# A macaron network on one core: causal mask by VectorE, one product per scan tile, dt rows by group

## The chip, the cores and the metric

The kernel runs on one core of one Trainium2 chip. TensorE (PE in the profile) multiplies matrices, VectorE (DVE), ScalarE (ACT) and GpSimd (POOL) work elementwise, and nearly all transfers are issued from the queue of SyncE (SP). Each engine carries out its own instructions in the order in which they stand in its queue and waits at semaphores for the others. Time is the device time of one execution in microseconds (us); lower is better. Before the change the median of three runs was 1147.51 us.

## The reference

The input x has 4 batches of 512 tokens with 128 features. Six layers follow one another, each with a residual connection and a layer norm without weights in front:

```
x = x + 0.5 * tree_attention(layernorm(x))   # three 16-leaf tree MLPs give q, k, v; softmax attention
x = x + attention(layernorm(x))              # 16 heads of 8 features, RoPE, ALiBi, causal
x = x + 0.5 * tree_attention(layernorm(x))
x = x + 0.5 * experts(layernorm(x))          # 8 experts, top 2, and a shared one
x = x + mamba(layernorm(x))                  # selective scan, 256 channels, 16 states
x = x + 0.5 * experts(layernorm(x))
```

Two places matter here. In the causal attention the scores of keys after the query are replaced by a very negative number before the softmax:

```
scores = scores + slopes[:, None, None] * rel
scores = where(causal, -1e9, scores)
attn = softmax(scores)
```

In the scan each of 256 x 16 states obeys, along the 512 tokens,

```
dA = exp(dt[t] * A)
h  = dA * h + (dt[t] * x[t]) * B[t]
y  = sum over the 16 states of h * C[t]
```

## The kernel before, in words

One batch is four tiles of 128 tokens; most tiles are 128 partitions by 512 (`S`) fp32 elements. The work of each layer and batch is a Python generator that yields after each small step. `Job` objects give every step a due time from the table `TIMES` (`h0` to `h3` for the causal heads, `s0` to `s3` for the scan, `T`, `t`, `e`, `f` for trees and experts), and the steps are emitted in the order of those due times. So the heads of one batch are interleaved with trees and experts of others, and the scan of one batch with experts and trees of others. The framework that the kernel is written in then settles the order on each engine and inserts the semaphores. `work(role)` takes the next of `BUFS[role]` rotating SBUF buffers, `bank(role)` the next of `BANKS[role]` PSUM banks.

**Causal heads.** `head_consts` (L474) makes four stacks of queries (`qs`, role `q_bias`) and two of keys (`ks`, role `k_bias`), each filled with 1.0 by GpSimd (L480) and then given bias rows by DMA and ScalarE. `head_stack` (L526) moves the high and low parts of q and k into rows 24 to 119 of them, and `head_maxima` (L576) puts the negated row maxima into rows 120 to 127 of the query stacks, so that one matmul gives scores with ALiBi and with the maximum subtracted. `head_keys` (L536) makes, on GpSimd, four masked copies of the keys, one per head. `head_scores` (L546) runs a first round of score matmuls into the one bank of role `head_max` (L557) and lets VectorE take the masked row maximum (L565). `head_mix` (L590) runs the second round into two banks of role `head_sc` (L633), for four key tiles kt: queries before the key tile are left out, so that a view holds one head of 512 columns (kt=0), one of 384 (kt=1), two of 256 (kt=2) or four of 128 (kt=3), eleven views for each of 16 quarters (4 batches x 4), 176 views. In each view the first 128 columns of a head are the diagonal block. A matmul of an identity with a constant triangle in bf16, `future_t`, adds a large negative number to the masked part of all diagonal blocks of the view (L641), ScalarE takes the exponential into a `pt` tile (L649), and four steps later (`LAG_MIX`) matmuls with the values follow (L601).

**Selective scan.** `state_prep` (L830) computes dt, dt*x and B, C and writes the rows of dt and dt*x to DRAM (`state_rows`). `state_main` (L925) covers each batch with two chunks c of 128 channels. For a chunk, eight DMAs (`spread`, L923) bring for each of four groups g of 32 channels the rows of dt and of dt*x back, each row copied to four partitions (one per state), into `dts` and `dtxs` tiles of 4 x 512; there are two of each. Then for q = 0 to 3 (four states each) a matmul spreads B into a bank (L958), and for each g: ScalarE makes the decay (L970, two banks), VectorE multiplies dt*x by B (L971), VectorE scans (L972), GpSimd multiplies by C (L973). The scanned tiles are single 128 x 512 buffers of role `states`, eight of them. Five steps later (`LAG_STATE`) four matmuls add the states up (`sums`, L930, L934). In all there are 4 batches x 2 chunks x 4 q x 4 g = 128 such steps.

The constants for the mask come in one bf16 tile, `whole` (L200 to L203), with the leaf paths of the trees, the identity, `future_t` and `future`.

## Time and profile before

| what | value |
|---|---|
| median of three runs | 1147.51 us (1146.84 to 1148.99) |
| the profiled execution | 1150.85 us, span 1149.1 us |
| mean granted TensorE clock | 0.988 |
| PE busy | 1080.6 us (94%) |
| DVE busy | 909.7 us (79%) |
| ACT busy | 517.1 us (45%) |
| POOL busy | 411.6 us (36%) |
| DMA | 146.42 MB, mean 127 GB/s |

The time of an execution holds 1.75 us more than the span from the first to the last instruction. The profiled execution is 3.34 us above the median of the runs. PE rows give matmuls with modelled ends that overlap; PEld rows are weight loads beside them. A group's row in the profile has the instruction's line, engine, operation and tiles, its count, its busy time and mean duration, and then the idle time of the engine just before it and what ended most of it. In a window's row each engine has its busy time in that stretch and the number of instructions.

### The profile page before, as it was taken

What the parts mean: (1) busy time and instruction counts of PE and PEld (TensorE: products, weight loads), DVE (VectorE), ACT (ScalarE), POOL (GpSimd) and SP (SyncE); (2) the same over time, 40 slices, a digit from 0 to 9 for tenths busy, and PEclk for the clock granted to TensorE, in tenths of its full rate; (3) what the DMA queues carried; (4) which work ended last, traced back from release to release, by engine and by line L of the source; (5) the groups of instructions that cost most, each with busy time, mean ns of one, the idle gap of its engine ahead of it and who ended that gap; (6) DMA issues with size and microseconds to landing.
All of it is one profiled execution on the core that took longest, in us unless ns stands there. A gap on an engine that the chain in (4) does not pass through costs nothing.

```text
span 1149.1 us, 16519 instructions
## 1 busy us (share of the span) xinstructions
PE 1080.6 (94%) x5536; PEld 715.5 (62%) x5536; DVE 909.7 (79%) x2199; ACT 517.1 (45%) x1078; POOL 411.6 (36%) x396
## 2 busy tenths in 40 slices
PE   3999999999999999999999999998798989998998
PEld 2666566566665667765566676675276656655677
DVE  5566787577676677776789998799989999999864
ACT  2221423233332455544533643565476567454444
POOL 4115322002100141320314651266626656656623
PEclk9999999999999999999999999999899999999999
DMA  7787755231442122333752334662038323823310
GB/s 208 203 248 215 260 137 122 75 94 57 85 139 60 54 58 60 104 85 112 232 181 90 125 84 122 234 210 92 1 98 278 127 60 125 292 74 124 111 51 10
DMA packets 79653, 146.42 MB, mean 127 GB/s; under 512 B 7537, under 2 KB 39665, under 8 KB 79569
## 3 DMA queue, kind: packets, MB, share of 16 engines
q1 hardware_dynamic: 79280, 145.07, 42.1%
q8 instruction: 44, 0.72, 0.3%
q14 instruction: 41, 0.33, 0.1%
q10 hardware_dynamic: 288, 0.30, 0.1%
HBM read 125.35 MB, written 13.70 MB: 121 GB/s over the span
## 4 chain that ended last, share of the span: by engine, by line
PE 63%; DVE 20%; issue 6%; DMA 4%; POOL 3%; ACT 3%; SPq 1%; POOLq 0%; ACTq 0%; DVEq 0%
PE tree_acc L404 11%; PE moe_acc L773 7%; DVE states L972 6%; PE head_acc L601 5%; PE tree_mm L173 4%; PE head_max L557 4%; PE head_sc L633 3%; PE moe L173 3%; PE tree_mm L175 3%; PE tree_mm L174 3%; DVE states L971 3%; PE moe L174 3%; PE moe L175 3%; DVE u L759 2%; PE state_acc L934 2%
## 5 line engine op out<-in xcount | busy, mean ns | idle before, releaser
L973 POOL TENSOR_TENSOR states<-states,cs 128x512 f32<-128x512 f32 x128 | 163.4, 1282 | 161.9 <-DVE states L972 93.1
L404 PE MATMUL tree_acc<-full,ring 128*128 128x512 f32 x384 | 194.3, 598 | 5.2 <-DVE full L394 4.9
L565 DVE CUSTOM_DVE_ANT_0 head_max<-head_max,kept 128x128 f32<-128x128 f32 (+3 forms) x256 | 126.8, 496 | 64.1 <-PE head_max L557 61.9
L394 DVE SCALAR_TENSOR_TENSOR full<-tree_mm,kept,mask 128x512 f32<-128x512 f32 x188 | 138.5, 746 | 40.2 <-PE tree_mm L175 35.1
L649 ACT ACTIVATE pt<-head_sc 128x512 f32<-128x512 f32 (+1 forms) x176 | 95.0, 559 | 139.0 <-PE head_sc L641 138.3
L972 DVE TENSOR_TENSOR_SCAN states<-decay,states 128x512 f32<-128x512 f32 x128 | 154.6, 1216 | 0.5
L773 PEld LDWEIGHTS moe_acc<-ring,u 128*128 128x128 f32 x1152 | 141.4, 193 | 17.6 <-DVE u L765 3.0
L773 PE MATMUL moe_acc<-ring,u 128*128 128x128 f32 x1152 | 145.7, 278 | 1.0 <-DVE u L759 0.7
L173 PE MATMUL moe<-xl,ring 128*128 128x512 f32 x288 | 128.8, 448 | 8.9 <-DVE u L765 1.9
L784 POOL TENSOR_TENSOR kept<-kept,y 128x512 f32<-128x512 f32 x64 | 83.4, 1303 | 136.2 <-ACT y L783 118.8
L970 ACT ACTIVATE decay<-dts,kept 128x512 f32<-128x512 f32 x128 | 88.4, 693 | 88.1 <-DVE states L972 66.5
L758 ACT ACTIVATE u<-moe 128x512 f32<-128x512 f32 x144 | 86.3, 602 | 70.4 <-PE moe L175 66.5
L759 DVE SCALAR_TENSOR_TENSOR u<-u,moe 128x512 f32<-128x512 f32 x144 | 97.0, 677 | 23.4 <-ACT u L758 23.1
L174 PE MATMUL moe<-xh,ring 128*128 128x512 f32 x288 | 115.4, 401 | 0.0
L175 PE MATMUL moe<-xh,ring 128*128 128x512 f32 x288 | 115.0, 400 | 0.0
L541 POOL TENSOR_SCALAR km<-k_bias,kept 128x512 fp32r<-128x512 f32 x64 | 43.3, 697 | 171.3 <-PE head_sc L633 151.0
L783 ACT ACTIVATE y<-moe_acc,scratch 128x128 f32<-128x128 f32 x256 | 73.3, 370 | 65.6 <-PE moe_acc L773 64.8
L173 PE MATMUL tree_mm<-xl,ring 128*128 128x512 f32 x188 | 96.1, 514 | 0.4 <-DVE full L394 0.2
L404 PEld LDWEIGHTS tree_acc<-full,ring 128*128 128x128 f32 x384 | 71.0, 190 | 35.8 <-issue 17.3
L173 PEld LDWEIGHTS moe<-xl,ring 128*128 128x128 f32 x288 | 54.8, 190 | 60.4 <-DVE u L765 10.4
L557 PE MATMUL head_max<-km,q_bias 120*128 120x512 f32 (+2 forms) x192 | 91.7, 479 | 0.5 <-POOL km L541 0.4
L971 DVE TENSOR_TENSOR states<-state_b,dtxs 128x512 f32<-128x512 f32 x128 | 85.6, 682 | 5.5 <-PE state_acc L934 2.6
(242 smaller groups left out, 1982.3 us busy)
## 6 DMA issues: line engine op xcount, KB each, us to landing
ring<-moe_parts SPq DMA_DIRECT2D x72, 512.0 KB
ring<-tree_parts SPq DMA_DIRECT2D x42, 512.0 KB
ring<-in_fff_w SPq DMA_DIRECT2D x24, 512.0 KB
mask<-fff_taken SPq DMA_DIRECT2D x48, 256.0 KB
ring<-in_moe_w SPq DMA_DIRECT2D x16, 512.0 KB
dts<-state_rows SPq DMA_DIRECT2D x32, 256.0 KB
dtxs<-state_rows SPq DMA_DIRECT2D x32, 256.0 KB
moe_parts<-moe_w SPq DMA_DIRECT2D x9, 512.0 KB
```

The lines of the kernel that those rows point to most:

```text
L173: nc.tensor.matmul(ps, lhsT=lh, rhs=rl, start=start, stop=False)
L174: nc.tensor.matmul(ps, lhsT=ll, rhs=rh, start=False, stop=False)
L175: nc.tensor.matmul(ps, lhsT=lh, rhs=rh, start=False, stop=stop)
L394: nc.vector.scalar_tensor_tensor(full, ps, neg_b1[:, n : n + 1], st.masks[k][:, c, :], ALU.max, ALU.mult)
L404: nc.tensor.matmul(acc, lhsT=weights[k][1][:, c, :], rhs=h, start=(c == 0), stop=False)
L557: nc.tensor.matmul(view, lhsT=qs[:R_MAX, g, ts(i, P)], rhs=km[j0 // 2][:R_MAX, j0 % 2 : j0 % 2 + each, :kw], start=True, stop=True,)
L565: nc.vector.tensor_tensor_reduce(view[:, n, :], view[:, n, :], future[:, S - kw :], -1.0, float(np.finfo(np.float32).max), ALU.add, ALU.mi ...
L759: nc.vector.scalar_tensor_tensor(u, u, 1.0, ps1, ALU.add, ALU.mult)
L773: nc.tensor.matmul(acc[:, ts(i, P)], lhsT=h[c][:, ts(i, P)], rhs=w2[:, e % 4 * 2 + c, :], start=(c == 0), stop=(c == 1),)
L971: nc.vector.tensor_mul(h, bs, dtx[:, g, :])
L972: nc.vector.tensor_tensor_scan(h, dA, h, 0.0, ALU.mult, ALU.add)
L973: nc.gpsimd.tensor_mul(h, h, cs[:, q])
```

## The change: what it does

Four edits are made together.

- The mask. The identity matmul is gone. The score matmuls of a view are each a group of their own (start and stop), and VectorE replaces the diagonal blocks in PSUM by their minimum with a bf16 constant, `at_most`, which is a large negative number where the key comes after the query and 2^127 elsewhere. `whole` loses the identity.
- The product. For each q one VectorE instruction multiplies all four groups of `dtx` (128 x 4 x 512) by the bank with B, broadcast over the groups, into a `states` tile of 4 x 512. There are three such tiles. The scan, the product with C and the sums work on slices of it.
- The dt rows. `dts` is one 128 x 512 tile per group, six of them. `dtxs` stays two tiles of 4 x 512.
- The stacks. The four query stacks are not filled with 1.0 first; the two key stacks are.

```diff
-    ... dtx=2, pos=2, dts=2, dtxs=2, states=8),
+    ... dtx=2, pos=2, dts=6, dtxs=2, states=3),
...
-    whole = keep((3 * P + S) // 2).bitcast(BF16)
+    whole = keep((2 * P + S) // 2).bitcast(BF16)
...
-    leafpath, ident_h, future_t = (whole[:, ts(k, P)] for k in range(3))
-    future = whole[:, 3 * P :]
+    leafpath, at_most = (whole[:, ts(k, P)] for k in range(2))
+    future = whole[:, 2 * P :]
...
-                nc.gpsimd.memset(stack.bitcast(F32), 1.0)
+                if lst is ks:
+                    nc.gpsimd.memset(stack.bitcast(F32), 1.0)
...
                         rhs=qs[:, g, kt * P :],
-                        start=(j == 0),
-                        stop=False,
+                        start=True,
+                        stop=True,
                     )
-                nc.tensor.matmul(
+                nc.vector.tensor_tensor(
                     view[:, :, :P],
-                    lhsT=ident_h,
-                    rhs=future_t.unsqueeze(1).to_broadcast([P, each, P]),
-                    start=False,
-                    stop=True,
+                    view[:, :, :P],
+                    at_most.unsqueeze(1).to_broadcast([P, each, P]),
+                    ALU.min,
                 )
...
-                    rhs=hs[g],
+                    rhs=hs[:, g, :],
...
-            dt, dtx = work("dts", (4, S)), work("dtxs", (4, S))
+            dt, dtx = [], work("dtxs", (4, S))
...
             for g in range(4):
-                for m, to in enumerate((dt, dtx)):
-                    spread(to[:, g, :], rows[m, g])
+                dt.append(work("dts"))
+                for m, to in enumerate((dt[g], dtx[:, g, :])):
+                    spread(to, rows[m, g])
...
-                hs = []
+                hs = work("states", (4, S))
+                nc.vector.tensor_mul(hs, dtx, bs.unsqueeze(1).to_broadcast([P, 4, S]))
                 for g in range(4):
                     k = (4 * c + g) * GROUPS + q
-                    dA, h = bank("decay"), work("states")
-                    hs.append(h)
-                    nc.scalar.activation(dA, dt[:, g, :], AF.Exp, scale=A[:, k : k + 1])
-                    nc.vector.tensor_mul(h, bs, dtx[:, g, :])
+                    dA, h = bank("decay"), hs[:, g, :]
+                    nc.scalar.activation(dA, dt[g], AF.Exp, scale=A[:, k : k + 1])
                     nc.vector.tensor_tensor_scan(h, dA, h, 0.0, ALU.mult, ALU.add)
...
     k_after_q = np.triu(np.full((P, P), -FAR, f), 1)
+    at_most = np.where(k_after_q.T < 0, f(-FAR), f(2.0**127))
```

In the order of instructions on the engines the rest stays nearly where it was: apart from what is added and removed, most groups move by fewer than twenty places in queues of 1000 to 4000. The largest move is that of the transposes of one tree preparation, which stand some 260 PE instructions later, still ahead of the matmuls that use them. On SP the eight row loads of a chunk stand as two of dt, four of dt*x, two of dt, and in second chunks the last two of dt stand behind five to eight further loads, mostly of expert weights.

More of the change, by code (lines that the diff above doesn't have):

```diff
@@ L102 @@
     **dict(moe_w=1, lgT=1, u0=4, u1=3, y=2, v3=3),
-    **dict(hid=1, xs=3, sz=2, conv=1, xd=1, xb=2, cs=1, dt=3, dtx=2, pos=2, dts=2, dtxs=2, states=8),
+    **dict(hid=1, xs=3, sz=2, conv=1, xd=1, xb=2, cs=1, dt=3, dtx=2, pos=2, dts=6, dtxs=2, states=3),
 }
@@ L1221, in _constants @@
         "whole": np.concatenate(
-            [leafpath, np.eye(P, dtype=f), k_after_q.T, np.zeros((P, S - P), f), k_after_q], axis=1
+            [leafpath, at_most, np.zeros((P, S - P), f), k_after_q], axis=1
         ).astype(ml_dtypes.bfloat16),
```

## The prediction

> **What bounds the kernel now.** I read the page first, then the busy time by stretch, then the waits of PE in the stretch of the causal heads, then groups and the timeline.

> ```profile
> span 1149.1 us, 16519 instructions
> ...
> PE   3999999999999999999999999998798989998998
> ...
> DVE  5566787577676677776789998799989999999864
> ...
> 130.00:585.00 455.00, 450.36 (x2454) 289.49 (x2455) 325.94 (x1034) 184.95 (x379) 87.51 (x115) 1.00 0.39 109
> 585.00:850.00 265.00, 249.62 (x1205) 161.63 (x1203) 244.87 (x492) 130.45 (x265) 120.24 (x101) 0.97 0.37 115
> 850.00:1090.00 240.00, 218.21 (x1132) 147.43 (x1131) 225.60 (x385) 142.21 (x300) 147.03 (x114) 0.99 0.46 151
> ```

> The masks run from 134.9 to 583.8 us, the scans from 565 to 1082 us. The columns of the windows are the length, then busy PE, PEld, DVE, ACT, POOL. Between 130 and 585 us PE is busy 99% and DVE 72%; from 585 to 1090 us DVE is busy 93% (470.5 of 505 us) and PE also 93%. So the heads' stretch is bound by PE, and the scans' by VectorE with PE close behind. Since matmul rows overlap, I checked how much of PE's time is waiting:

> ```profile
> PEld head_max L557 <- DVE scratch L565: 4.2, 10, 0.8
> PEld head_sc L633 <- ACT pt L649: 2.3, 7, 0.6
> PEld head_acc L601 <- ACT pt L649: 0.5, 1, 0.5
> ```

> In 130 to 585 us PE waits little for the other engines. The two places to watch are the one `head_max` bank, freed by VectorE, and the two `head_sc` banks, freed by the exponential.

> **The change part by part.**

> *Mask taken off PE.* The timeline of PE gives its price:

> ```profile
> 309.01 0.33 PE L633 MATMUL head_sc<-q_bias,km 128*128 128x384 f32 x1
> 309.18 0.23 PE L641 MATMUL head_sc<-kept 128*128 128x128 bf16 x1
> 309.22 0.47 PE L173 MATMUL tree_mm<-xl,ring 128*128 128x512 f32 x1
> 309.54 0.40 PE L174 MATMUL tree_mm<-xh,ring 128*128 128x512 f32 x1
> ```

> Read by ends: the mask ends 0.07 us after the scores (309.41 against 309.34), and the matmul behind it ends 0.28 us later where an L174 takes 0.23, so 0.05 us goes to a weight load that did not start early. Read so over all 176 masks, the step is 0.072 us for 128 columns (128 times), 0.126 for 256 (32) and 0.231 for 512 (16): 9.2 + 4.0 + 3.7 = 16.9 us, and with 0.05 for each mask (8.8 us) 25.7 us. PE is the bound there, so 17 to 26 us is what the edit can give. I take 21.

> *Minimum put on VectorE.* No row has a minimum in PSUM; the nearest are these, of which L565 reads and writes PSUM with a constant from SBUF as the minimum will:

> ```profile
> L565 DVE CUSTOM_DVE_ANT_0 head_max<-head_max,kept 128x128 f32<-128x128 f32 x64 | 18.8, 294 | 8.6 <-PE head_max L557 8.0
> L565 DVE CUSTOM_DVE_ANT_0 head_max<-head_max,kept 128x512 f32<-128x512 f32 x64 | 44.6, 697 | 26.8 <-PE head_max L557 26.3
> L620 DVE TENSOR_TENSOR o<-head_turn,scratch 128x128 f32<-128x128 f32 x16 | 4.6, 286 | 0.1
> L971 DVE TENSOR_TENSOR states<-state_b,dtxs 128x512 f32<-128x512 f32 x128 | 85.6, 682 | 5.5 <-PE state_acc L934 2.6 <-PE state_b L958 1.5 <-DMA dtxs<-state_rows 1.3
> ...
> 959.50 1.28 DVE L971 TENSOR_TENSOR states<-state_b,dtxs 128x512 f32<-128x512 f32 x2
> ```

> The last row shows two products in 1.28 us where each lasts 0.68: the second starts 0.60 us after the first. So there are two prices for an instruction, its duration (for whoever waits for it) and the step to the next one (for the engine). The steps read off the timeline for 128, 256 and 512 columns are 0.20, 0.33 and 0.60 us. VectorE gets 128 x 0.20 + 32 x 0.33 + 16 x 0.60 = 46 us more (by durations of 0.29, 0.42 and 0.69 us, 62). 326 us become 372, in a stretch of some 440: 85% in place of 72%. VectorE stays below PE, so this costs nothing as load, but it costs waits. What was a step of 0.07 us between scores and exponential becomes a semaphore, whatever VectorE is at, and 0.29 us. At the end of a mask VectorE has in the median 0.26 us left of its current instruction, and others can stand between; I take 0.7 us more until a `head_sc` bank is free. In the trace, the time from the exponential that frees a bank to the next score matmul in it is under 0.37 us for a tenth of the views and under 1.18 us for a fifth. So some 14% of 176 views, 25, would stop PE for about 0.4 us each: 10 us if nothing is made up later, and PE's whole queue, trees included, stands behind such a wait. Next, the second row maxima: an L565 behind a minimum frees the `head_max` bank 0.2 to 0.6 us later, and 30% of the 192 L557 have less than 0.22 us in hand. That is up to 58 x 0.2 = 12 us; a wait taken at one bank gives slack at the other, so I take half of the two together, 11 us. The heads' stretch comes to -21 + 11 = -10 us, with -26 (no waits) and +5 (all waits and the smaller saving) as ends.

> *One product for four.* Between 128 and 512 columns L565 grows by 697 - 294 = 403 ns, 1.05 ns a column. By the step, 512 columns take 0.60 us, of which 0.537 is for the columns and 0.063 fixed; 2048 columns are then 2.148 + 0.063 = 2.21 us. 32 x 2.21 = 70.7 against 128 x 0.60 = 76.8: -6 us. By durations (0.145 fixed) it is 32 x 2.29 = 73.4 against 87.3: -14. I take the step, since VectorE is nearly never idle there and successive instructions overlap. If nothing of it were fixed, the gain would be 0.

> [...]

> Against the gain stand three things. A VectorE instruction of 2.2 us blocks what is queued behind it, where now the longest is the scan (1.22 us); in 585 to 1090 us PE's weight loads wait 10.4 us for L765, 7.9 for L759 and 10.1 for scans, so expert matmuls wait there already. The scans lose the 0.60 us product between them while ScalarE (54% busy, 0.69 us a decay) must refill two `decay` banks: 96 scans times some 0.05 us is 5 us. And the first product of a chunk needs all of dt*x: in the third batch the first product started 871.37 on the landing of the first dt*x row load, and the fourth was issued 1.9 us after the first, so 4 chunks times up to 2 us. Three tiles of four hold twelve steps where eight did, which removes the 2.6 us of waits for `state_acc`. Sum: -6 - 2 + 5 = -3 us, with -14 and +12 (5, 8 and some PE waits, without gain) as ends.

> *dt rows.* The same 32 loads of 256 KB. Six tiles instead of eight slots make the last two loads of a second chunk wait for the exponentials of the first chunk, and they are queued on SP behind expert weights, which wait for matmuls. Cover: between issue and use lie at least four scan steps, some 10 us, against 4 to 5 us from issue to use for the row loads on the chain of waits. I put 0, and if that cover is gone a few us in each of four batches, inside the +12 above.

> *Stacks not preset.* Four fills by GpSimd of 0.95 us each at 0.7 us. They run while the first loads are under way; the first layer norm waits on ScalarE behind a weight cast that ran at 10.80 us on a DMA. 0; should that cast be early, at most the 2.3 us that L825 took on VectorE while GpSimd filled.

> **Sum.** -10 - 3 = -13 us. The profiled execution took 1150.85 us (span 1149.1 and 1.75 around it): 1137.9. It lies 3.3 us above the median shown, so against the median I forecast 1147.5 - 13 = 1134.5 us.

> **The rivals.**

> *VectorE's hop holds PE (slower).* Place: the two `head_sc` banks and the one `head_max` bank. The edit frees 17 to 26 us over 176 views, 0.10 to 0.15 us each. If PE waits longer than that per view on average, the gain is gone; at 0.25 us per view the stretch is 44 - 21 = +23 us, and with +0 in the scans the time is 1171. For it: one bank, small slack, 85% load on an engine that serves in order. Against it: in 585 to 850 us VectorE is busy 92% and PE still 94%.

> *Full gain.* The order on the engines leaves room for the minimum, the waits stay small, and VectorE's time in the scans falls by the durations: -26 - 12 = -38, 1110 us. For it: VectorE idles 129 us in the heads' stretch. Against it: the slack above.

> *Scans lose what heads gain.* The long product and the uncovered decays cost +12, heads -10: 1149 us, no change to slightly slower.

> **How the numbers follow.** A difference of 0.2% (2.3 us) is about what a measurement of this kernel can tell from no change. Forecast 0.47 (its own range 1117 to 1144), full gain 0.11, scans' loss 0.13, VectorE's hop 0.29. Faster: 0.47, 0.11 and a little of the third, less the upper edge of the first: 0.58. Same 0.08, slower 0.34. The range for 8 in 10 goes from 1110 (full gain) to 1167 (hop at 0.23 us per view).

> **What would show it.** In the heads' stretch the L641 rows are gone, PE's busy time falls by about 20 us or its waits for ACT pt and for DVE grow: `head_sc` waiting for ACT pt well above 2.3 us and `head_max` waiting for VectorE above 4.2 us mean the hop. The minimum should last 0.29, 0.42 and 0.69 us, and DVE be busy near 85%. The product should last 2.29 us and step 2.21; scans waiting for ACT decay (0.5 us of idle time now) above 5 us mean the lost cover. The last exponential should end about 10 us sooner than 584.2. I am wrong if PE's waits in the heads sum to over 20 us, or if the scans' stretch gets longer.

## The result and the profile after

The changed kernel took 1165.42 us (1164.6 to 1165.68) against 1147.45 us (1146.84 to 1148.99) of the kernel before on the same chip: a ratio of 1.0153, 95% interval 1.0136 to 1.0171, so 17.6 us slower on 1149. The prediction was 1134.5 us and faster. Its range held the time; its sign was wrong. The profiled execution took 1165.19 us, with a mean granted clock of 0.980 (0.988 before).

The page of the changed kernel, its span and the forty slices of PE and VectorE:

```profile
span 1162.2 us, 16178 instructions
...
PE   4999989999999989999999999998798989898998
...
DVE  5566788778786778877799997799889998989864
```

The same three stretches as before (length, then busy PE, PEld, DVE, ACT, POOL, granted clock, DMA share, GB/s):

```profile
130.00:585.00 455.00, 441.27 (x2226) 278.80 (x2225) 357.94 (x1170) 182.66 (x372) 86.77 (x115) 0.99 0.37 104
585.00:850.00 265.00, 249.65 (x1199) 162.76 (x1197) 237.80 (x447) 124.85 (x252) 120.24 (x102) 0.97 0.38 119
850.00:1090.00 240.00, 219.00 (x1105) 148.89 (x1105) 223.60 (x351) 143.64 (x304) 137.97 (x108) 0.97 0.43 142
```

In the heads' stretch VectorE went from 326 to 358 us and PE from 99% to 97% busy: PE, the bound, has gaps now, and in the same 455 us it got through 2226 instructions instead of 2454. (The changed kernel has 176 fewer of them in all.) In the scans' two stretches VectorE is busy less (461 us instead of 470), and the work is not done sooner: the last scan ends at 1093.1 us, 11.2 us later than before, and 8.2 us of that are there already when the last exponential of the heads ends.

The new and the merged instructions are as long as predicted. Groups of VectorE (line, shapes, count, busy us, mean ns, then idle time before them and what ended it):

```profile
L642 DVE TENSOR_TENSOR head_sc<-head_sc,kept 128x128 f32<-128x128 f32 x128 | 38.5, 308 | 11.2 <-PE head_sc L634 10.5
L642 DVE TENSOR_TENSOR head_sc<-head_sc,kept 128x256 f32<-128x256 f32 x32 | 13.5, 431 | 5.3 <-PE head_sc L634 4.6 <-ACT pt L649 0.7
L642 DVE TENSOR_TENSOR head_sc<-head_sc,kept 128x512 f32<-128x512 f32 x16 | 11.2, 700 | 0.1
L967 DVE TENSOR_TENSOR states<-dtxs,state_b 128x2048 f32<-128x2048 f32 x32 | 72.9, 2277 | 4.2 <-PE state_b L959 3.4 <-POOL states L973 0.4 <-POOL kept L784 0.3
L972 DVE TENSOR_TENSOR_SCAN states<-decay,states 128x512 f32<-128x512 f32 x128 | 153.8, 1210 | 2.0 <-ACT decay L971 1.9
```

PE's waits at the two places that I had told the reader to watch, and at a third (window 130 to 585 us; lines have moved by one: L634 are the scores, L558 the first round, L602 the matmuls with the values, L601 before, which I call the mix below):

```profile
PEld head_acc L602 <- issue: 21.8, 70, 0.8
PEld head_sc L634 <- ACT pt L649: 2.8, 7, 0.6
PEld head_max L558 <- DVE scratch L566: 0.9, 2, 0.7
```

The `head_sc` banks make PE wait 2.8 us where it was 2.3, the `head_max` bank 0.9 where it was 4.2. The loss is not there. What grew is the row of the mix, 70 times and 21.8 us; "issue" means that the profile shows nothing that it waited for, so no engine was late. In the kernel before the same row was:

```profile
PEld head_acc L601 <- issue: 6.9, 24, 0.6
```

**The mix stands in more pieces.** A mix is four matmuls into the four 32-row parts of one bank. Groups of PE, before and then after; every row has the same count and nearly the same mean:

```profile
L601 PE MATMUL head_acc<-pt,vv 128*32 128x512 f32 x128 | 24.3, 605 | 1.4 <-ACT vv L520 1.1 <-ACT pt L649 0.3
L601 PE MATMUL head_acc<-pt,vv 128*32 128x384 f32 x128 | 18.6, 498 | 0.0
L601 PE MATMUL head_acc<-pt,vv 128*32 128x256 f32 x128 | 12.0, 390 | 0.0
L601 PE MATMUL head_acc<-pt,vv 128*32 128x128 f32 x128 | 7.5, 283 | 0.0
```

```profile
L602 PE MATMUL head_acc<-pt,vv 128*32 128x512 f32 x128 | 28.5, 605 | 0.0
L602 PE MATMUL head_acc<-pt,vv 128*32 128x384 f32 x128 | 25.1, 504 | 1.8 <-ACT pt L649 1.8
L602 PE MATMUL head_acc<-pt,vv 128*32 128x256 f32 x128 | 13.2, 390 | 0.0
L602 PE MATMUL head_acc<-pt,vv 128*32 128x128 f32 x128 | 8.4, 284 | 0.9 <-ACT pt L649 0.9
```

Busy time rose from 62.4 to 75.2 us, though no matmul is longer: they overlap less. The timeline of PE after shows why (the rows count two records for each matmul, 128 for the 64 of one width: x8 are all four matmuls, x2 is one):

```profile
409.05 1.04 PE L602 MATMUL head_acc<-pt,vv 128*32 128x512 f32 x2
...
412.96 1.06 PE L602 MATMUL head_acc<-pt,vv 128*32 128x512 f32 x8
...
416.42 0.92 PE L602 MATMUL head_acc<-pt,vv 128*32 128x384 f32 x2 [1.80 <-ACT pt L649]
...
418.42 1.49 PE L602 MATMUL head_acc<-pt,vv 128*32 128x384 f32 x2
...
420.65 0.83 PE L602 MATMUL head_acc<-pt,vv 128*32 128x384 f32 x2
```

One matmul alone takes 1.04 us, four in a row take 1.06. The mix from 416.42 on stands in single pieces, and each piece costs what all four would. I call a run of these matmuls on PE with no other matmul between them a stretch (two mixes that follow one another make one), and count its cost from the end of the matmul before it to its own last end. Read so over the whole trace, four matmuls of one width in a row cost 0.36, 0.57, 0.78 or 1.00 us (128, 256, 384, 512 columns), and one alone only 0.02 us less. There are 64 mixes; before, they stand in 72 stretches and take 55.0 us of PE, after in 87 and take 67.9. That is 12.9 us of the 16.9 us that the 176 masks had taken by the same reading.

The 1.80 us in front of the third piece has a second price, in windows of the changed kernel around it (the granted clock is the third figure from the right):

```profile
410.00:416.00 6.00, 4.62 (x30) 3.01 (x29) 5.27 (x19) 2.21 (x5) 1.28 (x1) 1.00 0.44 92
416.00:422.00 6.00, 5.58 (x16) 2.44 (x16) 3.35 (x18) 2.46 (x6) 2.62 (x4) 0.72 0.31 66
```

After the gap the clock is at half for 3.41 us (417.0 to 420.4), and the piece at 418.42 takes 1.49 us instead of 0.83. There are two such stretches in the heads after (the other at 157.6, behind gaps of 1.44 and 1.83 us), none before. At half speed each costs half its length, 1.7 us, and the two 3.4 us: an estimate from the 3.41 us, as are all losses at half clock below.

### The profile page after: what moved, and what is told of

Read it like the earlier page. It is cut to its first block, busy times and chain, and to the rows that moved or that the text cites. A ratio compares the mean times of both kernels' runs of the same rounds, so it can differ in the third digit from the quotient of the medians.

```text
span 1162.2 us, 16178 instructions
## 1 busy us (share of the span) xinstructions
PE 1085.2 (93%) x5360; PEld 718.3 (62%) x5360; DVE 942.5 (81%) x2279; ACT 517.5 (45%) x1078; POOL 406.1 (35%) x392
## 5 line engine op out<-in xcount | busy, mean ns | idle before, releaser
L394 DVE SCALAR_TENSOR_TENSOR full<-tree_mm,kept,mask 128x512 f32<-128x512 f32 x188 | 138.2, 744 | 36.1 <-PE tree_mm L175 26.7
L649 ACT ACTIVATE pt<-head_sc 128x512 f32<-128x512 f32 (+1 forms) x176 | 95.6, 558 | 142.8 <-DVE head_sc L642 127.4
L773 PEld LDWEIGHTS moe_acc<-ring,u 128*128 128x128 f32 x1152 | 143.8, 194 | 17.9 <-issue 5.1
L173 PE MATMUL moe<-xl,ring 128*128 128x512 f32 x288 | 128.3, 447 | 11.7 <-DVE states L972 3.2
L971 ACT ACTIVATE decay<-dts,kept 128x512 f32<-128x512 f32 x128 | 87.7, 694 | 70.0 <-DVE states L972 56.2
L174 PE MATMUL moe<-xh,ring 128*128 128x512 f32 x288 | 114.9, 399 | 0.0
L759 DVE SCALAR_TENSOR_TENSOR u<-u,moe 128x512 f32<-128x512 f32 x144 | 97.0, 675 | 22.0 <-ACT u L758 21.6
L173 PE MATMUL tree_mm<-xl,ring 128*128 128x512 f32 x188 | 95.7, 512 | 5.6 <-DVE full L394 4.4
L558 PE MATMUL head_max<-km,q_bias 120*128 120x512 f32 (+2 forms) x192 | 91.8, 479 | 2.5 <-DVE scratch L271 1.4
L404 PEld LDWEIGHTS tree_acc<-full,ring 128*128 128x128 f32 x384 | 70.7, 190 | 35.9 <-issue 19.7
L173 PEld LDWEIGHTS moe<-xl,ring 128*128 128x128 f32 x288 | 54.6, 190 | 55.3 <-DVE states L972 6.6
L765 DVE TENSOR_TENSOR u<-u,moe 128x512 f32<-128x512 f32 x128 | 85.9, 674 | 2.8 <-DVE scratch L277 0.4
```

Source lines behind the costliest of these rows:

```text
L173: nc.tensor.matmul(ps, lhsT=lh, rhs=rl, start=start, stop=False)
L174: nc.tensor.matmul(ps, lhsT=ll, rhs=rh, start=False, stop=False)
L394: nc.vector.scalar_tensor_tensor(full, ps, neg_b1[:, n : n + 1], st.masks[k][:, c, :], ALU.max, ALU.mult)
L404: nc.tensor.matmul(acc, lhsT=weights[k][1][:, c, :], rhs=h, start=(c == 0), stop=False)
L558: nc.tensor.matmul(view, lhsT=qs[:R_MAX, g, ts(i, P)], rhs=km[j0 // 2][:R_MAX, j0 % 2 : j0 % 2 + each, :kw], start=True, stop=True,)
L649: nc.scalar.activation(pt, view, AF.Exp)
```

## The experiments

Times are set against the kernel before by their ratios, since its median lay between 1147.5 and 1150 us beside the different kernels; a ratio is turned into us on 1149. In the diffs, `...` leaves out unchanged lines. The theories of the first four: T1, VectorE's hop holds PE; T2, the scans lose; T3, every edit changes PE's order, and that costs.

### The parts of the change

**The mask edit alone** is the part of the diff with the minimum. 

> The kernel before with the mask edit alone: no identity matmul, the minimum on VectorE. T1 (VectorE's hop in front of the exponential holds PE, the mask edit carries the loss): 1157 to 1166 us, and the end-to-end time of the score, mix and tree matmuls between 130 and 600 us grows by some 15 us and more over the kernel before. T2 (the loss comes from the scan edit or the dt tiles): 1137 to 1147 us. T3 (neither by itself: every edit changes the order in which matmuls stand on PE, and the broken groups of four L601 matmuls cost the time): anything from 1140 to 1165, with a number of separate stretches of L601 nearer to 90 than to 72.

Measured: 1157.54 us, ratio 1.0077 (1.0062 to 1.0092), +8.8 us; the mix in 86 stretches, 67.5 us. Half of the loss, at the lower edge of T1's range and inside T3's, with the stretches that T3 named.

**The scan edits alone** are the product, the dt tiles and the buffers. 

> The kernel before with the scan edits alone: one product for four groups, a dt tile for each group, three state tiles of four. T1: within 3 us of the kernel before (1144 to 1150 us). T2: 1155 to 1163 us, with the scans ending 8 to 15 us later. T3: the difference to before and that of the mask edit alone do not add up to the 18 us of both.

Measured: 1155.74 us, ratio 1.0059 (1.0044 to 1.0074), +6.8 us. The two parts add up to 15.6 of the 17.6 us, so neither T1 nor T2 alone holds; there are two losses. The other 2 us are within the intervals of the three ratios; what the unfilled stacks do, which had no run of their own, and what the parts do to each other would be in them.

### What the masks had cost PE

```diff
-                nc.tensor.matmul(
-                    view[:, :, :P],
-                    lhsT=ident_h,
...
-                nc.scalar.activation(pt, view, AF.Exp)
+                nc.scalar.activation(pt, view, AF.Exp, bias=lower_by)
```

> The kernel before without the identity matmul and without any minimum; the exponential takes a constant bias of -40 instead. It leaves the causal mask out of the second round, so it computes less. It prices what the matmul held, without a hop to VectorE. T1: the whole 17 to 26 us come off, 1122 to 1131 us, and PE's waits in the heads stay as before. T3: much less than that comes off (1135 to 1150 us), because the groups of four L601 matmuls break up here too.

Measured: 1142.89 us, ratio 0.9955 (0.9939 to 0.9972), -5.2 us; 80 stretches. The bias as a tile made the exponential longer, 687 against 598 ns for 512 columns, so the 40 went into the table that L565 adds:

```diff
-            [leafpath, at_most, np.zeros((P, S - P), f), k_after_q], axis=1
+            [leafpath, at_most, np.full((P, S - P), 40.0, f), k_after_q + 40.0 * (k_after_q == 0)], axis=1
```

> As the kernel without any mask, but the 40 is added in the table of the second row maxima (L565 adds it at no cost) and not as a bias of the exponential, which made each exponential 0.09 us longer there (687 against 597 ns for 512 columns). It leaves the causal mask out of the second round. T1 (the identity matmuls held PE for 17 to 26 us): 1123 to 1132 us. T3 (what they gave back is paid again in broken groups and shorter cover): 1138 to 1144 us.

Measured: 1143.06 us, ratio 0.9949 (0.9933 to 0.9965), -5.9 us. The longer exponential had cost nothing that shows here. With no mask at all and nothing in its place, PE's 17 to 26 us shrink to 6: the mix went to 78 stretches and 59.0 us, the 0.05 us reloads did not come back as shorter steps of other matmuls, and PE, now further ahead, waits more elsewhere (between 130 us and the last exponential it is idle for 8.6 us, 4.6 before). So with these banks and this order the removal is worth 6 us, and the hop of the minimum costs 8.8 + 5.9 = 14.7 us on top. In the profiles the last exponential ends 7.4 us sooner than before without a mask and 8.9 us later with the minimum: 16.3 us, of which the mix takes 8.5 (59.0 to 67.5), half clock 3.4 (none to two stretches), and about 4 are left for waits at other matmuls. The split is rough: a piece of the mix that runs at half clock is in both of the first two.

### Whether the order of the mix carries it

The four matmuls kept together in the changed kernel:

```diff
-            for j in range(4):
...
-                nc.tensor.matmul(
+            with tc.high_priority():
+                for j in (3, 0, 1, 2):
...
+                    mm = nc.tensor.matmul(
...
+                    if j == 3:
+                        lead = mm
+                    else:
+                        tc.add_manual_dep(mm.ins, lead.ins.name, ...)
```

> The changed kernel, with the four L601-type mix matmuls of a step kept together on PE: the fourth is issued first, the other three wait in order behind it, and the four have high priority in the framework's order. Read by ends, a stretch of such matmuls costs PE 0.36, 0.57, 0.78 or 1.00 us (128, 256, 384, 512 columns) whether one, two, three or four stand in it; the changed kernel has 87 stretches for 67.9 us, whole they are 64 for 16 x (0.36 + 0.57 + 0.78 + 1.00) = 43.4 us. Theory 'broken groups': 24.5 us less than the changed kernel if all of it lies on the path, 1141 us; 1138 to 1149. Theory 'hop' (PE stands for the exponential, and the broken groups only fill such waits): the waits come back in front of the groups, 1155 to 1166 us.

Measured: 1152.97 us, ratio 1.0028 (1.0006 to 1.005): 14.4 us less than the changed kernel by the ratios, with a wide spread (1148.35 to 1159.21). The mix stands in 61 stretches and takes 51.6 us. That lies between the two theories: in this profile broken groups were most of the loss in the heads (the last exponential ends 1.0 us before that of the kernel before, where it was 8.2 us behind), but the mix now waits for its last exponential itself, the scores' steps grew by 5 us, and PE ran at half clock for 24 us between 130 and 590 us (mean granted clock 0.97, 12 us lost; in the changed kernel 6.8 and 3.4), which took back part of it.

The same edit on the kernel before: 

> The kernel before with the same edit to the mix: 72 stretches for 55.0 us become 64 to 65 for 43.4. Theory 'broken groups': 11.6 us less than the kernel before, 1137 us (1134 to 1142). Theory 'hop': PE hardly waits in the kernel before, so about the same 1137 to 1148.

Measured: 1154.93 us, ratio 1.0053 (1.0034 to 1.0073), +6.1 us: a miss for both theories. The mix fell from 55.0 to 48.1 us and the last exponential came 2.6 us sooner, as wanted; 5 to 6 us were then lost at 690 to 766 us, the place that the scan edits lose at too (below).

The minimum done twice, in the mask edit alone:

```diff
+                nc.vector.tensor_tensor(
+                    view[:, :, :P], view[:, :, :P],
+                    at_most.unsqueeze(1).to_broadcast([P, each, P]), ALU.min,
+                )
```

> The mask edit alone with the minimum done twice in a row (the second changes nothing), so VectorE's part between scores and exponential is 0.20 to 0.60 us longer. Theory 'order': the mix matmuls stand in 115 stretches in place of 86; 29 more at a mean of some 0.8 us are 23 us, so 1172 to 1185 us, and the waits of head_sc for the exponential stay small. Theory 'banks' (PE waits for the head_sc banks): 1162 to 1170 us, 176 x 0.05 us more, with the waits of head_sc for ACT pt above 10 us.

Measured: 1210.06 us, ratio 1.0536 (1.0504 to 1.0567), +61.6 us, far above both ranges. The mix stands in 115 stretches and takes 92.4 us, 24.9 more than in the mask edit alone, as 'order' said. But the banks now count as well, in the waits of PE (130 to 600 us):

```profile
PEld head_acc L601 <- issue: 23.3, 76, 0.8
PEld head_sc L633 <- ACT pt L654: 16.2, 27, 1.6
PEld head_acc L601 <- ACT pt L654: 7.7, 11, 1.9
PE head_sc L633 <- ACT pt L654: 4.3, 5, 1.2
```

So the wait at the two `head_sc` banks that I predicted exists; it comes with twice the hop, not with one.

More banks, first on the mask edit alone:

```diff
-... head_max=1, ... head_sc=2, ...
+... head_max=2, ... head_sc=3, ...
```

> The mask edit alone with three head_sc banks and two head_max banks in place of two and one. Theory 'banks': the 10 us and more that the minimum cost come back, 1141 to 1148 us. Theory 'order': 78 stretches in place of 86, some 6 to 8 us, so 1148 to 1153 us.

Measured: 1155.23 us, ratio 1.0057 (1.0035 to 1.008), 2.3 us less than the mask edit alone, which the two intervals do not tell from no change; 78 stretches, 59.6 us. 'Banks' falls: a third bank does not bring 10 us back. 'Order' was right on the 8 us of the mix (67.5 to 59.6) and wrong on how much reaches the end: half clock in the heads rose from 3.4 to 8.5 us lost (mean granted clock 0.98 in 130 to 590 us).

> The kernel before with three head_sc banks and two head_max banks. Theory 'banks': PE hardly waits there, so the same within 3 us (1146 to 1152 us). Theory 'order': 66 stretches in place of 72, 51 of them whole, some 5 us less, 1141 to 1146 us.

Measured: 1146.81 us, ratio 0.9977 (0.9963 to 0.9991), -2.6 us; 66 stretches, 47.5 us. The direction of 'order', a third of the 7.5 us that the mix gave up; the figure itself lies just outside the range of 'order' and inside that of 'banks'.

In the last two runs, and at the last exponential of the kernel before with its mix kept whole, about a third of what the mix gave up came through. So the stretches say where PE's time went, and not how much of it a repair returns.

### The mask behind the exponential

GpSimd multiplies the diagonal blocks of `pt` by 0 or 1, where no PSUM bank waits:

```diff
+                nc.gpsimd.tensor_mul(
+                    pt[:, :, :P], pt[:, :, :P],
+                    at_most.unsqueeze(1).to_broadcast([P, each, P]),
+                )
```

> The kernel before without the identity matmul; the exponential takes a constant bias of -40, which cancels in the division by the row sum, and GpSimd then multiplies the diagonal blocks of its result in SBUF by 0 or 1. The hop stands behind the exponential, where no PSUM bank waits for it. T1: the head_sc banks come free as in the kernel before, and the mix has LAG_MIX steps in hand, so 1124 to 1140 us. T3: as without any mask, within 5 us of that kernel. If GpSimd's step (an estimate of 0.5 to 1.5 us from its other rows) makes the mix late: above 1150 us.

Measured: 1151.46 us, ratio 1.0023 (1.0009 to 1.0037), +2.6 us; 84 stretches. Above T1's range and T3's, and inside the last of the three, in which GpSimd's step makes the mix late. Without the bias tile: 

> The mask by GpSimd behind the exponential, with the 40 in the table of the maxima and no bias on the exponential. If the longer exponential cost the earlier GpSimd kernel its gain: 1138 to 1146 us, some 8 us less. If not: 1147 to 1153 us as with the bias.

Measured: 1147.61 us, ratio 0.9986 (0.9972 to 1.0), -1.6 us; 82 stretches, 62.0 us. The time lies in the range for 'if not', near its edge: some 4 us went with the longer exponential, half of the 8 expected. That fits a mix that has GpSimd to wait for behind it, which no run shows by itself; without a mask the longer exponential had cost nothing. Then the banks and the `pt` tiles with which the mix breaks less:

```diff
-    **dict(pt=6, mixed=2, o=3, oT=2),
+    **dict(pt=8, mixed=2, o=3, oT=2),
...
-... head_max=1, ... head_sc=2, ...
+... head_max=2, ... head_sc=3, ...
```

> The mask by GpSimd behind the exponential (the 40 in the table of the maxima), with three head_sc banks, two head_max banks and eight pt tiles. The mix matmuls stand in 67 stretches in place of 82 of the GpSimd kernel before it. Theory 'order': 15 stretches at some 0.8 us come off, 1136 to 1143 us, and so faster than both kernels. If only half of it reaches the end, as with the kernel before with more banks: 1141 to 1146 us. If the order is not what limits it: 1146 to 1150 us.

Measured: 1138.63 us (1135.56 to 1139.1), ratio 0.9893 (0.9876 to 0.991): 12.3 us faster than the kernel before and some 30 us faster than the changed one, inside the range of 'order'. Its heads' stretch and its mix of 512 columns:

```profile
130.00:585.00 455.00, 446.83 (x2350) 291.32 (x2349) 334.79 (x1052) 189.89 (x393) 184.06 (x293) 1.00 0.40 115
...
L601 PE MATMUL head_acc<-pt,vv 128*32 128x512 f32 x128 | 21.2, 604 | 0.6 <-ACT vv L520 0.6
```

One stretch of 3.41 us at half clock is left in the heads (at 170.9 us; it rounds away in the 1.00), where the changed kernel had two; the mix takes 53.6 us by ends in 67 stretches, and PE starts 2350 instructions in these 455 us. The last exponential ends 14.3 us before that of the kernel before, close to the 16.9 us of steps that the masks had held. The banks alone had given 2.6 us and this mask alone 1.6, so the two together give more than their sum. The run changes order, banks, tiles and clock together, so it shows that the gain can be had, and not which of them has how much of it.

### What the scan edits lose

> The kernel before with a dt tile for each group alone (six tiles), products as before. Theory 'long block': no difference, 1146 to 1151 us. Theory 'tiles': 1152 to 1158 us.

Measured: 1149.61 us, ratio 1.0002 (0.9988 to 1.0016). The dt tiles cost nothing that shows.

Two products of two groups in place of one of four:

```diff
-                nc.vector.tensor_mul(hs, dtx, bs.unsqueeze(1).to_broadcast([P, 4, S]))
+                for k in range(2):
+                    two = slice(2 * k, 2 * k + 2)
+                    nc.vector.tensor_mul(hs[:, two], dtx[:, two], bs.unsqueeze(1).to_broadcast([P, 2, S]))
```

> The scan edits alone, but the product in two instructions of two groups (1024 columns, an estimate of 1.14 us a step by the slope of 0.537 us for 512) in place of one of 2.2 us. Theory 'long block' (the 2.2 us product stands before the short tree chain L327, L350, L355, whose end came 5 us later at 685 us): most of the 7 us comes back, 1147 to 1152 us. Theory 'tiles' (three state tiles of four or six dt tiles cost it): as the scan edits alone, 1154 to 1158 us.

Measured: 1158.84 us, ratio 1.0082 (1.006 to 1.0105), +9.4 us. The length of the block is not the cause.

Four state tiles (`states=4`): 

> The scan edits alone with four state tiles of four groups (sixteen steps) in place of three. Theory 'tiles' (a tile is free only when all four gathers have read it): most of the 7 us comes back, 1147 to 1151 us. Theory 'order' (the long product changes where the framework puts the other VectorE work, the tree's L355 at 685 us above all): 1153 to 1158 us as before it.

Measured: 1157.47 us, ratio 1.0073 (1.0048 to 1.0097), +8.4 us. Nor is the number of tiles: a fourth brings nothing back.

Four products, each still in front of its own scan, into a shared tile:

```diff
-                nc.vector.tensor_mul(hs, dtx, bs.unsqueeze(1).to_broadcast([P, 4, S]))
...
+                    nc.vector.tensor_mul(h, bs, dtx[:, g, :])
                     nc.vector.tensor_tensor_scan(h, dA, h, 0.0, ALU.mult, ALU.add)
```

> The scan edits alone, with the product left as four instructions of 512 columns that write the four parts of a shared state tile; three tiles. Theory 'tiles': 1153 to 1158 us, as the scan edits. Theory 'order' by the product: 1147 to 1151 us, as the kernel before.

Measured: 1150.9 us, ratio 1.0012 (1.0003 to 1.0022), +1.4 us. Tiles and sharing cost at most that.

The same four products of 512 columns, all in front of the four scans:

```diff
-                nc.vector.tensor_mul(hs, dtx, bs.unsqueeze(1).to_broadcast([P, 4, S]))
+                for g in range(4):
+                    nc.vector.tensor_mul(hs[:, g, :], bs, dtx[:, g, :])
```

> The scan edits alone with four products of 512 columns, all four in front of the four scans of a step. Theory 'merge' (the instruction of 2048 or 1024 columns itself costs the time): 1147 to 1152 us. Theory 'ahead' (products done before the scans that need them push the scans and what else stands in VectorE's queue back): 1154 to 1160 us.

Measured: 1157.88 us, ratio 1.0085 (1.0061 to 1.0109), +9.8 us. Nothing is merged here, and the loss is all there.

One product of 1024 columns in front of each two scans:

```diff
+                    if g % 2 == 0:
+                        two = slice(g, g + 2)
+                        nc.vector.tensor_mul(hs[:, two], dtx[:, two], bs.unsqueeze(1).to_broadcast([P, 2, S]))
                     nc.vector.tensor_tensor_scan(h, dA, h, 0.0, ALU.mult, ALU.add)
```

> The scan edits alone, with a product of 1024 columns right in front of each two scans, so that one product at most runs ahead. Theory 'ahead': between the products in place (1150.9 us) and two products in front (1158.8 us): 1151 to 1155 us. Theory 'merge': as two merged products in front, 1157 to 1160 us.

Measured: 1155.07 us, ratio 1.0047 (1.0027 to 1.0067), +5.4 us, between the two as 'ahead' said, at the upper edge of its range. So the loss is the products' place: done ahead of the scans that need them, on an engine that is 93% busy there.

It starts around 690 us, after the last of the eight tree preparations (L355 to L363). With the scan edits alone the 32nd scan ends 1.1 us later than before (687.1 us), the 40th 6.4 us (before 765.5), the last 3.6; with the products first 0.6, 5.9 and 5.7; with the products in place -1.5, 1.6 and -1.6. VectorE's timeline and the loads of the masks, of the kernel before, and then of the scan edits alone:

```profile
680.19 0.69 DVE L355 TENSOR_SCALAR taken<-tree_tr 48x512 uint8<-48x512 f32 x1
...
683.48 2.76 SPq L363 DMA_DIRECT2D mask<-fff_taken  x4
...
690.12 0.75 DVE L394 SCALAR_TENSOR_TENSOR full<-tree_mm,kept,mask 128x512 f32<-128x512 f32 x1 [0.39 <-DMA mask<-fff_taken]
```

```profile
674.46 2.26 DVE L967 TENSOR_TENSOR states<-dtxs,state_b 128x2048 f32<-128x2048 f32 x1
676.64 0.67 DVE L327 TENSOR_TENSOR xl<-tree_tr,xh 128x512 fp32r<-128x512 f32 x1
...
685.15 0.68 DVE L355 TENSOR_SCALAR taken<-tree_tr 48x512 uint8<-48x512 f32 x1
...
690.81 2.64 SPq L363 DMA_DIRECT2D mask<-fff_taken  x4
...
696.38 0.75 DVE L394 SCALAR_TENSOR_TENSOR full<-tree_mm,kept,mask 128x512 f32<-128x512 f32 x1 [1.85 <-DMA mask<-fff_taken]
```

L355 makes the choice of tree leaves that goes to DRAM and comes back as masks. It ends 5 us later (4.4 with the products first, none with them in place), its masks are loaded from 690.81 instead of 683.48 us, and VectorE then stands 1.85 us for them at L394, with the layer norms of the next stages (L284 to L302) in its queue behind it: the L276 that the next L277 builds on had ended at 694.53, and that L277 started at 697.05, behind the L394. The kernel before with the mix kept whole lost at the same place: L355 was on time there (678.43), but from the store of the choice to the first L394 it took 12.2 us in place of 9.2, with two loads of 512 KB issued between the store and the masks, and VectorE stood 2.10 us. This chain is read from the traces: no run gave L355 its old place with the products still ahead, and with the products in place the first L394 still came 2.1 us later than before. What else in VectorE's queue moved behind the products was not separated by a run.

## Why the prediction was wrong

- **What bounds it.** Right: PE in the heads, VectorE with PE in the scans.
- **"Mask taken off PE ... 17 to 26 us is what the edit can give. I take 21."** This is the step that failed first. The 16.9 us of steps are gone, but 6 us came to the end. I took PE's queue as fixed but for the masks. The framework settles it anew, and the mix, whose price depends on what stands beside it, took 12.9 us of the 16.9 back in the changed kernel (4.0 without any mask, where PE's idle time took 4.0 more). The 8.8 us of reloads did not show as a gain. I had compared the orders and written that most groups move by fewer than twenty places; one place is enough to break a mix. The stretches can be counted in the program before it runs, as the later expectations did (115, 78, 66 and 67, as found).
- **"Minimum put on VectorE."** Steps and durations were right: 0.308, 0.431, 0.700 us against 0.29, 0.42, 0.69, and about 0.20, 0.33, 0.60 from one end to the next. The load was a little high, 79% in place of 85%. The cost, 11 us between 0 and 22, measured 14.7; but "25, would stop PE for about 0.4 us each" at the `head_sc` banks and "up to 58 x 0.2" at the `head_max` bank were the wrong places, 2.8 and 0.9 us. It came as broken mixes, half clock and waits of PE elsewhere. My test, waits of PE above 20 us, would not have caught it: waits named at PE's matmuls for VectorE and ScalarE in 130 to 585 us rose from 4.2 to 12.1 us only. (Those named at the weight loads, which run beside matmuls, were above 20 us before the change already: 39.1 us, then 57.2.) The other sign, a longer scans' stretch, hardly showed either: from the first scan to the end of the last one it was 514.6 us before and 515.6 after.
- **Heads, -10 in all.** Measured +8.8 for the mask edit, outside the ends of -26 and +5. The last exponential was to end about 10 us sooner and ended 8.2 us later in the changed kernel (584.2 us, named there as its end, is its start; it ended at 584.8).
- **"One product for four."** The step was 2.20 us (2.21 predicted) and the duration 2.28 (2.29 predicted), so VectorE got the 6 us of the term (32 x 2.20 = 70.4 us for 76.8). The +5 for refilling the decays did not come: scans waited 1.9 us for ScalarE. "A VectorE instruction of 2.2 us blocks what is queued behind it" named the right queue and the wrong property: halves lose as much, and so do four unmerged products, if they are ahead. -3 was predicted, +6.8 measured, inside -14 and +12, but the time did not go where the +12 was drawn from.
- **dt rows, 0.** Right, 0.2 us, within the noise. **Stacks, 0.** Not measured alone; they would be in the 2 us that the two parts leave, which is within the noise.
- **The rivals.** "VectorE's hop holds PE", 1171, was nearest in time, and wrong on where PE is held. That the range held 1165 us is luck: it reached so far for the sake of waits at the banks, and those did not come. The third came true in part in the size of the scans' loss (+6.8 of its +12), and neither in its cause there nor for the heads. The slower side deserved more than 0.34: with PE 99% busy in the heads, and PE and VectorE both 93% busy behind them, there were few places where a later result would have been harmless.

## What to carry to other kernels

When PE's queue is settled by a framework, removing a matmul also reorders those beside it; count in how many stretches the packed 32-column matmuls stand before and after, since one cost nearly as much as four here (0.02 us less). An operation can move to another engine where nothing waits for a bank, behind the exponential and not in front of it, but even there the gain came only with more banks and tiles, with which the packs broke less (12.3 us with 67 stretches, 1.6 us with 82). On an engine that serves in order and is 93% busy, work done ahead of its use cost time although no work was added (9.8 us here): merge only what is needed at the same moment.

## What the runs showed of the hardware that was not expected

- A gap of PE of 1.80 us in the heads was followed by 3.41 us at half clock, and a mix piece of 0.83 us took 1.49. A gap of 1.08 us in the kernel before, at 417 us, was not followed by half clock (granted clock 1.00 from 417 to 421 us). In the changed kernel with the mix kept whole such stretches cost 11.9 us in the heads, by the estimate above. The length of the gap does not decide it alone. In the kernel before a gap of 1.53 us was followed by half clock; with the scan edits alone one of 2.31 us was not (PE's timeline, then the window, of each):

```profile
935.71 0.50 PE L958 MATMUL state_b<-xb,rounded 128*128 128x512 f32 x1 [1.53 <-DVE u L765]
...
936.50:939.90 3.40, 3.40 (x9) 2.35 (x8) 3.40 (x6) 2.02 (x5) 2.37 (x2) 0.50 0.00 0
```

```profile
697.19 0.50 PE L173 MATMUL tree_mm<-xl,ring 128*128 128x512 f32 x1 [2.31 <-DVE full L394]
...
690.00:710.00 20.00, 17.46 (x86) 11.83 (x85) 15.09 (x53) 5.55 (x12) 5.05 (x7) 1.00 0.61 163
```

```profile
L649 ACT ACTIVATE pt<-head_sc 128x512 f32<-128x512 f32 x112 | 64.7, 598 | 99.3 <-PE head_sc L641 98.7
...
L644 ACT ACTIVATE pt<-head_sc,kept 128x512 f32<-128x512 f32 x112 | 74.1, 687 | 97.3 <-PE head_sc L635 97.1
...
L642 ACT ACTIVATE pt<-head_sc 128x512 f32<-128x512 f32 x112 | 64.2, 598 | 110.8 <-PE head_sc L633 110.4
```
